# Four graph layers on one NeuronCore: the running count along an adjacency row as one scan of 1024 columns instead of two of 512

## Chip, cores and metric

The kernel runs on one core of a Trainium2 chip. The metric is the device time of one execution in microseconds, as the median of several runs. One further execution was recorded by the hardware profiler. Engines are named as the profile names them: PE is TensorE's matmul, PEld its weight load, DVE is VectorE, ACT is ScalarE, POOL is GpSimd, and SP is SyncE, which here only issues DMAs.

## What is computed

Sixteen graphs of 1024 nodes with 128 features pass through four layers, each followed by a residual sum and a layer norm: masked attention (layer 0), an edge convolution that takes a maximum over the neighbours (layer 1), a graph isomorphism layer (layer 2), and three SAGE convolutions on a "dilated" adjacency (layer 3). The change is in the dilation, which depends on the adjacency alone:

```python
def step(carry, n):                      # n = 0 .. 1023, one graph
    row = jnp.take(carry, n, axis=0)
    nbi = row.astype(jnp.int32)
    num = jnp.sum(nbi)
    sf = jnp.where(num > T_DIL, (num + K_DIL - 1) // K_DIL, 1)   # T_DIL 10, K_DIL 2
    rank = jnp.cumsum(nbi)
    rm = row & (rank % sf == 0)
    valid = (mask_b[n] != 0) & (num > 1)
    rm = jnp.where(valid, rm, False)
    keep = ~rm
    carry = carry.at[n].set(row & keep)
    carry = carry.at[:, n].set(carry[:, n] & keep)
    return (carry, None)
```

Rows are treated in order, and what a row removes is removed from the column too, so it affects the rows that follow. `rank` is the running count of neighbours along the row.

## The kernel before

**The main loop.** Layers 0 to 2 and the dilation run in one loop of 16 x 86 = 1376 slots of two half-slots each. Layer 1 sets its frame. The neighbours' maximum is computed over groups of six neighbours by tables of all subsets. In `slot`, each half-slot does the same: `look_up` (L779) multiplies a table by one-hot columns into the PSUM tile `pg`, which has two buffers; `count` (L748, L749) prepares the one-hot columns of two slots later on PE and ACT; every second slot `table` and `low_part` (L760 to L770) prepare tables; and DVE takes the running maximum, `nc.vector.tensor_max(own, own, pg)` (L831), which sets a buffer of `pg` free.

**The order.** The instructions of PE, ACT, DVE and POOL are put down in the order in which this Python loop emits them. The layers' other work is written as generators ("streams") that ask for an engine with an estimated cost; `advance` lets them emit when that engine's account has room. The account of DVE gains 1.1 a half-slot up to 2.2. A request that gives a PSUM bank back, or that is marked urgent (the subset tables, `tables_of`, L463 and L467), goes ahead whatever the account says. After the streams, in the same half-slot, the dilation is asked for its next step if it is due (L816 to L819); its cost is taken off DVE's account. The maximum of the half-slot comes last.

**The dilation** (L481 to L683) treats rows in 32 blocks of 32. Partition `g*32 + r` holds row `r` of the block in four graphs (`Q` = 4), so that a block is `E[128, 4, 1024]` in 8-bit integers. For each block:

- `rest` and `low_counts` (L601, L603) start a chain of 31 steps on GpSimd (L616 to L626) that decides row by row, for the 16 graphs, what the rows of the block remove among themselves. The chain yields 1.03 slots a step and hands out one item of other work for DVE with each: `yield 1.03, next(work, 0), False` (L627). When the items run out, the steps go on without any.
- The items are those of `behind`, which is `remove` of the block before, and then those of `prepare` for the next block. `prepare` (7 items) cuts squares out of the next rows, subtracts the columns that were removed before (`gone_T`) and counts.
- The chain's result goes through DRAM (`hit`, `hit_p`, L631 to L636). Some 8.8 slots after the last step, DVE transposes it (`hit_T`, L639), takes it out of `E`, and computes each row's count and three factors, `centre`, `scale` and `width` (L640 to L658). Then follow the columns that the next block needs at once (L660 to L678), and the next block's sums (L587 to L603).

`remove` (L549 to L576) does the removal along whole rows. For each of the four row groups `q` it makes the running count (`rank`) on DVE by two scans, the second starting at the last value of the first; ACT turns the count into |scale * rank + centre| in place (L564); DVE compares that with `width` and multiplies by the row (`gone`, L567); SP writes `gone` to DRAM (`removed`, L569); DVE transposes it in 32 x 32 blocks (`last_T`, L572), and SP writes that to DRAM too (`removed_T`, L574). `gone` of row group q-1 comes after the scans of row group q. Each scan, each `gone` and each transpose is an item of its own: 16 a block. `rank` and `gone` have two buffers each.

**After the loop** come the last items of `remove`, the end of layer 2 for the last graph, and layer 3, whose edges are read from `removed` (`load_edges`).

Of the kernel before, what the change touches and what calls it, by code (L numbers as in the profile page):

```python
# [35 lines left out]
ALU = mybir.AluOpType  # L36
# [35 lines left out]
def tile_graph_layers(ctx: ExitStack, tc, a, out):  # L72
    nc = tc.nc
    x, adj, adjT = a["x"], a["adj"], a["adjT"]
    halves = (slice(0, 512), slice(512, 1024))
# [91 lines left out]
    for b in range(B):  # L167
        q, g = divmod(b, G)
# [67 lines left out]
    def layers_012():  # L236
# [244 lines left out]
        def dilation():  # L481
# [67 lines left out]
            def remove(k, E, centre, scale, width):  # L549

                nonlocal last_T
                own = slice(k * R, (k + 1) * R)
                after = K - 2 - k
                if after > 0:
                    last_T = dil.tile([P, Q, after, R], BF, name="last_T")
                ranks = [None] * Q
                for q in range(Q + 1):
                    if q < Q:
                        rank = ranks[q] = dil.tile([P, N], F32, name="rank", bufs=2)
                        for h, s in enumerate(halves):  # L560
                            nc.vector.tensor_tensor_scan(rank[:, s], E[:, q, s], E[:, q, s],
                                                         rank[:, 511:512] if h else 0.0, op0=ALU.add, op1=ALU.max)
                            yield 1.3
                        nc.scalar.activation(rank, rank, AF.Abs, bias=centre[:, q:q + 1], scale=scale[:, q:q + 1])  # L564
                    if q:
                        gone = dil.tile([P, N], BF, name="gone", bufs=2)
                        nc.vector.scalar_tensor_tensor(gone, ranks[q - 1], width[:, q - 1:q], E[:, q - 1, :],  # L567
                                                       op0=ALU.is_equal, op1=ALU.mult)
                        nc.sync.dma_start(out=removed[k, :, q - 1, :], in_=gone)  # L569
                        yield 1.3  # L570
                        if after > 0:
                            nc.vector.transpose(last_T[:, q - 1].rearrange("p k r -> p (k r)"), gone[:, (k + 2) * R:])  # L572
                            if after > 1:
                                nc.sync.dma_start(out=removed_T[k + 3:, :, q - 1, own].rearrange("k p r -> p k r"),  # L574
                                                  in_=last_T[:, q - 1, 1:])
                            yield 0.8  # L576
# [5 lines left out]
            for k in range(K):  # L582
                E, V, _, counts = this
# [76 lines left out]
                if k + 1 < K:  # L660
# [18 lines left out]
                    yield 0.5, 2.6, False  # L679
                    this = following  # L680
                behind = remove(k, E, centre, scale, width)
            for cost in behind:
                yield 0.5, cost, False  # L683
# [486 lines left out]
```

## Time and profile before

| what | value |
|---|---|
| median of 3 runs | 6616.1 us (6615.68 to 6616.88) |
| profiled execution, its own time | 6613.2 us |
| span of its instructions | 6611.5 us |
| main loop, from the first running maximum to the end of the last | 137.3 to 5281.4 us |
| running maxima (L829 and L831) | 2752 |
| scans of 512 columns (L561) | 256 |

The profile's page gives for each engine its busy time, its share of the span and its number of instructions, and then the span in 40 slices with the busy share of each in tenths (9 is 90% or more); a slice here is 165 us. A group's row has the line, the engine, the operation, output and inputs, the shape and the count; then its busy time in us and the mean of one instruction in ns; then the engine's idle time before these instructions in us, and what ended it. In the source view of one line the durations are minimum, median and maximum in ns, followed by the first and last start in us. The waits view has who waited for whom, the total in us, how often, and the longest. The timeline has start and length in us; `x2` are two instructions in a row, merged; idle time before it stands in brackets. The stretches view has the busy time of each engine in given stretches of the span, and their sum and mean.

### The profile page before, as it was taken

The numbers are of one execution on the slowest core, as the hardware profiler recorded it, in microseconds if no ns is written. First come the engines' busy times: TensorE is split into PE (matmuls) and PEld (weight loads), VectorE is DVE, ScalarE is ACT, GpSimd is POOL, SyncE is SP. The second block draws the span as 40 slices with busy tenths as digits, with TensorE's granted clock in tenths as the row PEclk, the third lists the DMA queues.
The fourth block names the chain that finished last, engine by engine and source line by source line (L and its number), as shares of the span: only waits on it lengthen the run. The fifth ranks groups of instructions, "written<-read, shape, count | busy, mean of one in ns | idle before, by whom it ended". The sixth has DMA issues, their size and how long they took to land. (4 is left out here: it accounts for less than half of the span.)

```text
span 6611.5 us, 85916 instructions
## 1 busy us (share of the span) xinstructions
PE 5697.7 (86%) x27306; PEld 2883.8 (44%) x27306; DVE 5317.7 (80%) x8130; ACT 3733.9 (56%) x6537; POOL 3844.7 (58%) x11285
## 2 busy tenths in 40 slices
PE   6989898989898989899888898888888768787986
PEld 3434344444444444444444444444443345555643
DVE  3989899999999999999999999999998834444453
ACT  4656566666666666666666656666655523333841
POOL 2675767676767776766666676767676511110126
PEclk8989898989898989898989899999987779888997
DMA  5121212121212121212112212121110156563635
GB/s 37 14 27 22 30 24 36 20 27 26 28 28 27 27 27 26 28 26 31 28 29 30 27 26 27 26 27 28 25 25 9 32 93 120 105 124 102 230 128 166
DMA packets 478381, 317.02 MB, mean 48 GB/s; under 512 B 301162, under 2 KB 429668, under 8 KB 473828
## 3 DMA queue, kind: packets, MB, share of 16 engines
q0 software_dynamic: 105648, 84.20, 14.6%
q1 hardware_dynamic: 367600, 226.13, 11.7%
q8 instruction: 214, 3.51, 0.2%
q10 hardware_dynamic: 4676, 1.19, 0.1%
q14 instruction: 243, 1.99, 0.1%
HBM read 412.71 MB, written 117.18 MB: 80 GB/s over the span
## 5 line engine op out<-in xcount | busy, mean ns | idle before, releaser
L831 DVE TENSOR_TENSOR best<-best,pg 128x1024 f32<-128x1024 f32 x2720 | 3234.4, 1210 | 309.0 <-PE pg L779 300.5
L749 ACT ACTIVATE hot<-pm,one_less 128x512 fp32r<-128x512 f32 x2752 | 1882.3, 688 | 1115.1 <-PE pm L748 1102.9
L779 PE MATMUL pg<-hot,high 64*128 64x512 f32 x5504 | 1479.1, 534 | 453.6 <-DVE best L831 417.8
L779 PE MATMUL pg<-hot,low 64*128 64x512 f32 x5504 | 1173.3, 423 | 0.0
L748 PE MATMUL pm<-AT,lit 120*128 120x512 fp8e4 x2752 | 1143.8, 416 | 9.3 <-ACT hot L749 6.2
L779 PEld LDWEIGHTS pg<-hot,high 64*128 64x128 f32 x5504 | 547.9, 196 | 1265.1 <-DVE best L831 792.4
L616 POOL TENSOR_SCALAR sc<-low_counts,half_mask,rest 16x1 f32<-16x1 f32 x992 | 435.7, 439 | 399.6 <-DVE rest L603 305.8
L779 PEld LDWEIGHTS pg<-hot,low 64*128 64x128 f32 x5504 | 573.4, 205 | 0.0
L748 PEld LDWEIGHTS <-lit 120*128 120x128 fp8e4 x2752 | 274.5, 100 | 624.8 <-issue 560.8
L621 POOL TENSOR_SCALAR sc<-sc 16x1 f32<-16x1 f32 x992 | 430.1, 434 | 105.0
L770 ACT CAST low<-pt 128x256 fp32r<-128x256 f32 x688 | 255.6, 371 | 396.3 <-PE pt L768 392.1
L980 POOL TENSOR_TENSOR length<-length,mhalf 128x8 f32<-128x8 f32 x48 | 78.9, 1644 | 571.7 <-DVE length L979 571.7
L618 POOL TENSOR_SCALAR sc<-sc 16x1 f32<-16x1 f32 x992 | 341.8, 345 | 107.7
L624 POOL TENSOR_SCALAR last_rank<-V,sc 16x31 f32<-16x31 bf16 (+30 forms) x992 | 387.1, 390 | 0.0
L623 POOL TENSOR_SCALAR hit<-V,sc 16x31 bf16<-16x31 bf16 (+30 forms) x992 | 372.5, 376 | 0.0
L768 PE MATMUL pt<-high,less 128*128 128x256 f32 x688 | 303.2, 441 | 66.3 <-ACT high L763 58.9
L467 DVE TENSOR_TENSOR sub<-sub,q 128x24 f32<-128x24 f32 (+11 forms) x768 | 306.6, 400 | 24.6 <-ACT q L289 10.5
L619 POOL TENSOR_SCALAR sc<-sc 16x1 f32<-16x1 f32 x992 | 270.1, 272 | 83.3
L937 ACT CAST m<-near 128x1024 fp32r<-128x1024 fp8e4 x256 | 253.3, 1044 | 112.7 <-DVE near L906 59.8
L760 PE MATMUL pt<-ident,sub 128*128 128x128 f32 x1376 | 293.9, 298 | 24.7 <-ACT hot L749 22.0
L377 PE MATMUL pav<-v,eT 128*128 128x128 f32 x2048 | 307.6, 296 | 2.1 <-ACT eT L370 2.1
L617 POOL TENSOR_SCALAR sc<-sc 16x1 f32<-16x1 f32 x992 | 256.6, 259 | 86.6
(258 smaller groups left out, 9495.7 us busy)
## 6 DMA issues: line engine op xcount, KB each, us to landing
removed<-gone SPq DMA_DIRECT2D x128, 256.0 KB
An<-in_adj_dram POOLq DMA_DIRECT2D x16, 1024.0 KB, 15.1
E<-in_adj_dram POOLq DMA_DIRECT2D x128, 128.0 KB, 6.8
gone_all<-removed POOLq DMA_DIRECT2D x64, 256.0 KB, 12.1
near<-in_adjT_dram POOLq DMA_DIRECT2D x16, 1024.0 KB, 17.3
h<-x SPq DMA_DIRECT2D x32, 512.0 KB
kept<-near SPq DMA_DIRECT2D x16, 1024.0 KB
share<-share SPq DMA_DIRECT2D x32, 512.0 KB
```

What stands on the lines that cost most here:

```text
L377: nc.tensor.matmul(pav, eT[:, c, :], values[b][:, c, :], start=(c == 0), stop=(c == T - 1))
L467: nc.vector.tensor_max(sub[:, :n_g, n:2 * n], sub[:, :n_g, 0:n], qg[:, 2 * g0:2 * g0 + n_g, k:k + 1].to_broadcast([P, n_g, n]))
L616: gp.tensor_scalar(half, mine, half_mask[:, m], rest[:, n:n + 1], op0=ALU.mult, op1=ALU.add)
L618: gp.tensor_scalar(sf, half, 5.5, sf, op0=ALU.is_gt, op1=ALU.mult)
L621: gp.tensor_scalar(to, at, sf, none, op0=ALU.subtract, op1=ALU.subtract)
L623: gp.tensor_scalar(hit[:, n, n + 1:], V[:, n, n + 1:], at, None, op0=ALU.is_equal)
L624: gp.tensor_scalar(last[:, n + 1:], V[:, n, n + 1:], to, None, op0=ALU.is_le)
L748: nc.tensor.matmul(pm, lit[:, r, :], AT[b * (T + 1) + c][:, halves[h]], start=True, stop=True)
L749: nc.scalar.activation(hots[s][:, halves[h]], pm, AF.Relu, bias=one_less)
L768: nc.tensor.matmul(pt, less, high, start=False, stop=True, skip_group_check=True)
L779: nc.tensor.matmul(pg[:, a], part[rows, at * P:(at + 1) * P], hots[s][rows, halves[h]], start=(k == 0), stop=(k == 1))
L831: nc.vector.tensor_max(own, own, pg)
```

## The change

In `remove`, the two scans over 512 columns, each an item of its own with a cost of 1.3, become one scan over 1024 columns with a cost of 2.3. The scan of a row group starts at zero, and there is no second one that reads the first one's last value. Nothing else is changed.

```diff
                 for q in range(Q + 1):
                     if q < Q:
                         rank = ranks[q] = dil.tile([P, N], F32, name="rank", bufs=2)
-                        for h, s in enumerate(halves):
-                            nc.vector.tensor_tensor_scan(rank[:, s], E[:, q, s], E[:, q, s],
-                                                         rank[:, 511:512] if h else 0.0, op0=ALU.add, op1=ALU.max)
-                            yield 1.3
+                        nc.vector.tensor_tensor_scan(rank, E[:, q, :], E[:, q, :], 0.0, op0=ALU.add, op1=ALU.max)
+                        yield 2.3
                         nc.scalar.activation(rank, rank, AF.Abs, bias=centre[:, q:q + 1], scale=scale[:, q:q + 1])
```

## Prediction

> **What bounds the kernel now.** I read the page first, then the dilation's own line, then the timeline of the main loop, then stretches of it, then the waits. Durations are in us unless marked ns.
>
> ```profile
> PE 5697.7 (86%) x27306; PEld 2883.8 (44%) x27306; DVE 5317.7 (80%) x8130; ACT 3733.9 (56%) x6537; POOL 3844.7 (58%) x11285
> PE   6989898989898989899888898888888768787986
> DVE  3989899999999999999999999999998834444453
> L831 DVE TENSOR_TENSOR best<-best,pg 128x1024 f32<-128x1024 f32 x2720 | 3234.4, 1210 | 309.0 <-PE pg L779 300.5
> ```
>
> The DVE row holds 8 or 9 from the second slice to the 32nd: the main loop, 137 to 5281 us, with 2752 half-slots, each with one running maximum (L831). DVE and PE are both near full there, so which of them waits has to be read by stretch. The dilation works in 32 blocks of 85.4 half-slots. I cut 26 of them (blocks 4 to 29) at three marks of the timeline: from `rest` (L603) to the last handed-out step of `remove` and `prepare`; from there to `hit_T` (L639); from there to the next `rest`. The sums of the three answers of the stretches view:
>
> ```profile
> core 0: us, PE busy (x) PEld busy (x) DVE busy (x) ACT busy (x) POOL busy (x), PEclk, DMA share, GB/s
> ...
> sum 2302.40, PE 2059.16 PEld 992.65 DVE 2226.55 ACT 1431.48 POOL 1938.40; mean PE 79.20 PEld 38.18 DVE 85.64 ACT 55.06 POOL 74.55
> ...
> sum 1505.30, PE 1414.78 PEld 680.49 DVE 1275.71 ACT 1047.22 POOL 962.21; mean PE 54.41 PEld 26.17 DVE 49.07 ACT 40.28 POOL 37.01
> ...
> sum 350.90, PE 234.13 PEld 111.37 DVE 332.70 ACT 115.95 POOL 22.80; mean PE 9.00 PEld 4.28 DVE 12.80 ACT 4.46 POOL 0.88
> ```
>
> By the starts of the maxima these hold 1176, 911 and 133 half-slots. In the **item stretch** DVE is busy 97%: 1.958 us a half-slot, idle (2302.4 - 2226.6) / 1176 = 0.064. In the **free stretch**, where the dilation gives DVE nothing, PE is busy 94% and DVE 85%: 1.652 us a half-slot, idle (1505.3 - 1275.7) / 911 = 0.252. So DVE sets the pace while it has items, and TensorE when it has none. The waits of DVE in the main loop say the same, and name a third bound:
>
> ```profile
> DVE best L831 <- PE pg L779: 300.5, 571, 6.7
> DVE hit_T L639 <- DMA hit_p<-hit: 54.2, 9, 11.1
> ```
>
> Nine blocks end in a wait for `hit_p`, the result of GpSimd's chain of 31 steps (L616 to L626). The timeline shows one:
>
> ```profile
> 2641.97 18.79 DVE L831 TENSOR_TENSOR best<-best,pg 128x1024 f32<-128x1024 f32 x16 [0.47 <-PE pg L779]
> 2666.51 0.31 DVE L639 STREAM_TRANSPOSE hit_T<-hit_p 128x128 bf16<-128x128 bf16 x1 [5.75 <-DMA hit_p<-hit]
> ```
>
> DVE runs sixteen maxima and then stands 5.75 us. In those blocks neither DVE nor PE decides, but the chain (2524.9 to 2654.8 in this one, by GpSimd's timeline) and some 11 us of DMA behind it. The nine are odd blocks; the even ones have some 12 us to spare there.
>
> **What the Trainium skill says.** "DVE: opcode table, instruction layouts, handler registers and perf-mode slots", section "6. Datapath and trigger behaviour": the built-in scan runs at half throughput. The trace agrees: (1206 - 425) ns over 384 more elements (rows below) is 2.03 ns an element, twice the 1.04 of a 0.96 GHz clock ("VectorE: DVE Perf Modes", section "Specifications"). "Perfetto Trace Analysis", section "Optimizing Scalar/DVE Operations": an instruction on SBUF carries about 60 ns, larger operations help a saturated engine, and where DVE isn't saturated but makes bubbles elsewhere, breaking instructions up helps. Both halves of that bear here. "SBUF — State Buffer", section "Who interferes with whom": a DVE instruction with two SBUF inputs shuts out a GpSimd instruction that reads SBUF, for its whole length. The trace agrees: the chain's L617 has a median of 224 ns and a longest of 1365, and such long ones lie in scans.
>
> **The change, part by part.** The rows of the old scans, one of a short scan, and a piece of timeline:
>
> ```profile
> L561 DVE TENSOR_TENSOR_SCAN rank<-E x128: 1195/1206/1275, 292.6 to 5258.6; 128x512 f32<-128x512 uint8 x128
> L561 DVE TENSOR_TENSOR_SCAN rank<-E,rank x128: 1255/1275/1330, 295.8 to 5260.8; 128x512 f32<-128x512 uint8 x128
> L668 DVE TENSOR_TENSOR_SCAN at_columns<-running,near_columns x31: 423/425/426, 285.6 to 5099.4; 128x128 f32<-128x128 bf16 x31
> ```
>
> ```profile
> 2531.95 1.21 DVE L561 TENSOR_TENSOR_SCAN rank<-E 128x512 f32<-128x512 uint8 x1
> 2533.08 2.32 DVE L831 TENSOR_TENSOR best<-best,pg 128x1024 f32<-128x1024 f32 x2
> 2535.32 1.27 DVE L561 TENSOR_TENSOR_SCAN rank<-E,rank 128x512 f32<-128x512 uint8 x1
> 2536.52 2.32 DVE L831 TENSOR_TENSOR best<-best,pg 128x1024 f32<-128x1024 f32 x2
> ```
>
> (1) DVE time. The next instruction starts before a scan's recorded end: a first half occupies DVE for 2533.08 - 1.95 = 1.13, a second for 2536.52 - 5.32 = 1.20. No scan of 1024 is in the trace. I add 512 elements at 2.03 to 2.08 ns to the first half's 1.13: 2.17 to 2.20; I take 2.20. A pair then saves 1.13 + 1.20 - 2.20 = 0.13 (ends: 0.13 and, by recorded durations, 0.22). Four pairs a block: **-0.52**.
>
> (2) Four half-steps fewer. The chain hands out one item with each of its steps, 1.03 slots or 2.06 half-slots apart. `remove` has 16 items a block and will have 12; `prepare` keeps its 7. Block boundaries don't move, because the 31 steps and the waits after them are fixed in slots. So 4 x 2.06 = 8.24 half-slots a block pass from the item stretch (45.2 a block) to the free one (35.0). Work saved on DVE turns into time saved only where DVE decides, and these half-slots now go at TensorE's pace. At the idle rates above this adds 8.24 x (0.252 - 0.064) = +1.55. Against it, the shortened item stretch is denser (its mean item is larger), so its idle may fall: 37 half-slots x up to 0.02 = -0.74. Sum with (1): +0.29 to +1.03; I take **+0.75** a block that DVE and PE decide.
>
> (3) The long scan itself. Queued behind it on DVE is one maximum, and behind that PE's look-up two half-slots later, since `pg` has two buffers. PE fills both and stands a microsecond longer. That is free while DVE is the later of the two, as it is among items; the cover gone, each long scan costs up to its second half, 1.07.
>
> (4) GpSimd. By the timeline an operation of the chain caught in a scan loses on average 0.956 of the scan's 1.24, that is all but 0.285. Two halves cost 1.91, one scan of 2.26 would cost 1.975: +0.06, four times a block: **+0.25** where the chain decides.
>
> (5) At no cost: the Abs on ACT (1.23 us) gets its whole row at once, and `gone` still comes a slot (3.5 us) or more after it. The DMAs of `removed` and `removed_T` on SP come one step earlier per row group after the first; SP stood waiting for `gone` 2012.9 us in all, so nothing queues before them. If they piled up, only `gone`'s two buffers would feel it, 3 steps apart. The planner books 2.3 instead of 2.6 for DVE; its running-maximum and table streams don't look at that account. After the last block the rest of `remove` shrinks from 12 half-slots to 8: about +1, as PE decides the four freed.
>
> Sum: 31 blocks run `remove` inside them. 22 x 0.75 = 16.5; the nine that wait for `hit_p`: 9 x 0.25 = 2.3; the end 1. Together +20 on the profiled execution's 6613.2 (span 6611.5 and 1.7 around it): 6633. The median of the runs is 2.9 higher: **6636**.
>
> **Rivals.** (R1) Faster. If the freed half-slots have so little matmul work that PE passes them at DVE's pace, no idle is added, and (1) stands alone: 22 x 0.52 = 11, by durations 22 x 0.88 = 19; 6597 to 6605, say 6600. It decides below the idle x at which -0.52 + 8.24 (x - 0.064) = 0, x = 0.127, half of what the free stretch shows. The sixteen maxima above (1.17 apart) speak for it; but that is the end of an odd block, after PE's other work has run out, and the freed half-slots lie at the beginning of the stretch. The nine blocks bound by GpSimd give no gain. (R2) Both cancel: the denser item stretch returns all of the idle, 6618. (R3) Much slower: PE is busy 89% of the item stretch too; if PE loses 0.4 of the extra 1.07 in each of 124 long scans and doesn't recover it, +50: 6666. Against it: DVE's idle there is 0.064 a half-slot.
>
> **The numbers.** My forecast 0.55, with its own range of 6622 to 6658; R1 0.08; R2 0.25; R3 0.12. About 0.2% (13 us) is what a measurement can tell from no change. R2, and 0.05 of my forecast's lower edge, lie within it: same 0.30; slower 0.62; faster 0.08. The range of 8 in 10 takes R2, part of R1 and part of R3: 6606 to 6662.
>
> **What would show it.** Scans: x128, near 2.26 us, 2.20 to the next start. DVE busy less by 17 to 28 in all. In the same cut of stretches: some 37 half-slots of items and 43 free ones a block, free idle near 0.25, item idle 0.04 to 0.06, and DVE's wait for `pg` up from 300 by about 35. The longest of the chain's GpSimd operations about 2.3 us. I am wrong if the free idle falls below 0.13 (faster), if the item stretch's idle rises (R3), or if the scan's time isn't linear in its length.

## The result, and the profile after

The changed kernel takes 6673.9 us (median of 4 runs, 6668.4 to 6676.4) against 6616.5 for the kernel before on the same chip: a ratio of 1.0092, 95% interval 1.0078 to 1.0105. The forecast was 6636 with a range to 6662: the sign was right, and the loss is almost three times the one forecast. The profiled execution took 6676.4 us, with a span of 6674.7.

The page after (line numbers behind the scan are two lower than before):

```profile
PE 5719.4 (86%) x27306; PEld 2892.4 (43%) x27306; DVE 5319.2 (80%) x8002; ACT 3742.4 (56%) x6537; POOL 3873.8 (58%) x11285
...
L829 DVE TENSOR_TENSOR best<-best,pg 128x1024 f32<-128x1024 f32 x2720 | 3239.7, 1211 | 387.6 <-PE pg L777 375.2
```

DVE runs 128 instructions fewer and is no less busy (5317.7 before). Its idle time before the running maxima rose from 309.0 to 387.6, nearly all of it a wait for `pg`. The source view of the scan, and the sums of the same three cuts of blocks 4 to 29 (items, free, end of block):

```profile
L560 DVE TENSOR_TENSOR_SCAN rank<-E x128: 2262/2272/2361, 292.2 to 5321.1; 128x1024 f32<-128x1024 uint8 x128
```

```profile
sum 1912.50, PE 1674.49 PEld 787.00 DVE 1839.14 ACT 1143.09 POOL 1623.53; mean PE 64.40 PEld 30.27 DVE 70.74 ACT 43.97 POOL 62.44
...
sum 1910.20, PE 1770.16 PEld 865.93 DVE 1613.24 ACT 1301.49 POOL 1299.18; mean PE 68.08 PEld 33.31 DVE 62.05 ACT 50.06 POOL 49.97
...
sum 406.70, PE 290.88 PEld 140.52 DVE 383.88 ACT 157.74 POOL 22.78; mean PE 11.19 PEld 5.40 DVE 14.76 ACT 6.07 POOL 0.88
```

The scan is what was forecast, and so are the half-slots of the first two stretches, 35.4 and 43.5 a block by the starts of the maxima. But the idle of the item stretch rose from 0.064 to 0.080 a half-slot, and the third stretch, which the change wasn't thought to touch, grew from 350.9 to 406.7 us with the number of its half-slots, from 133 to 168. So I took the time of each block from the timeline, from one `spread` to the next:

| block | before | after | change |
|---|---|---|---|
| 3 | 167.1 | 157.6 | -9.5 |
| 5 | 153.4 | 176.2 | +22.8 |
| 7 | 154.2 | 171.2 | +17.0 |
| 9 | 155.9 | 175.7 | +19.8 |
| the 27 others of blocks 0 to 30 | | | +12.3 in all |

Three blocks (5, 7 and 9) carry +59.6 of the +62.4. Here is the beginning of block 5 in the timeline, before:

```profile
933.75 0.26 DVE L590 TENSOR_TENSOR spread<-counts,of_graph 128x96 f32<-128x96 f32 x1
933.92 2.35 DVE L831 TENSOR_TENSOR best<-best,pg 128x1024 f32<-128x1024 f32 x2
936.19 0.17 DVE L601 COPY low_counts<-pc 16x32 f32<-16x32 f32 x1
```

and after:

```profile
925.32 0.26 DVE L588 TENSOR_TENSOR spread<-counts,of_graph 128x96 f32<-128x96 f32 x1
...
950.43 0.18 DVE L599 COPY low_counts<-pc 16x32 f32<-16x32 f32 x1 [0.39 <-PE pc L595]
...
950.63 2.27 DVE L560 TENSOR_TENSOR_SCAN rank<-E 128x1024 f32<-128x1024 uint8 x1
```

From `spread` to `low_counts` it is 2.4 us before and 25.1 after, 15 half-slots instead of 2. No engine waits there for long: the bracket shows 0.39 us in which DVE stood idle for the matmul into `pc`. The wait lies in the order itself: between the two, the dilation asks for a bank of the shared PSUM pair (`pc`). The two banks are handed out in turn, and when the planner wrote the order down, the one whose turn it was had gone to a long sum for layer 2 (`pa`, L419). PE's timeline has the 24 matmuls of that sum ahead of those of `pc`, and in between short uses of the banks by streams that the planner asks before the dilation:

```profile
925.49 1.47 PE L419 MATMUL pa<-An,parts 128*128 128x512 fp8e4 x6
...
941.41 0.82 PE L419 MATMUL pa<-An,parts 128*128 128x512 fp8e4 x3
...
949.80 0.52 PE L595 MATMUL pc<-of_row,spread 128*16 128x32 f32 x12
```

In blocks 7 and 9 such a sum stands at the same place. The chain on GpSimd starts that much late. The planner's due times don't move with it, so that the next steps are emitted one a half-slot instead of one in two, until they have caught up. Sixty half-slots on, this is what it does to the engines. Pieces of the timelines of GpSimd, of ACT and of PE, and a line of the waits from 1030 to 1060 us:

```profile
1035.14 0.30 POOL L616 TENSOR_SCALAR sc<-sc 16x1 f32<-16x1 f32 x1
1037.70 0.20 POOL L220 TENSOR_TENSOR ln_mv<-ln_st 128x8 f32<-128x8 f32 x1
```

```profile
1041.30 1.65 ACT L270 ACTIVATE X<-y,ln_mv 128x128 f32<-128x128 f32 x4 [10.03 <-POOL ln_mv L228]
```

```profile
1043.58 0.69 PE L758 MATMUL pt<-ident,sub 128*128 128x128 f32 x2 [10.40 <-ACT hot L747]
```

```profile
DVE best L829 <- PE pg L777: 16.6, 7, 10.8
```

A layer norm (`ln_mv`, L220 to L228) stands on GpSimd behind steps of the chain that were emitted in a clump. ACT, in order, reaches the norm's result 10 us early and stands; the one-hot columns behind it on ACT are late; PE stands 10.4, DVE 10.8. In blocks 7 and 9 ACT stands 10.2 and 11.3 us for `ln_mv`, and in each of the three blocks a second time, for 2.6 to 3.3. This wait over the main loop, before and after:

```profile
ACT X L270 <- POOL ln_mv L228: 9.5, 3, 7.7
...
ACT X L270 <- POOL ln_mv L228: 48.5, 7, 11.3
```

The six waits of blocks 5, 7 and 9 make up some 41 us; what else the three blocks lose wasn't followed to single waits. They have 88.7 us of DVE idle between them, against 32.0 before; in the whole main loop it rose by 66.5.

### The profile page after: what moved, and what is told of

Same layout as the page of the kernel before. It is cut to its first block, busy times and chain, and to the rows that moved or that the text cites. A ratio compares the mean times of both kernels' runs of the same rounds, so it can differ in the third digit from the quotient of the medians.

```text
span 6674.7 us, 85818 instructions
## 1 busy us (share of the span) xinstructions
PE 5719.4 (86%) x27306; PEld 2892.4 (43%) x27306; DVE 5319.2 (80%) x8002; ACT 3742.4 (56%) x6537; POOL 3873.8 (58%) x11285
## 5 line engine op out<-in xcount | busy, mean ns | idle before, releaser
L829 DVE TENSOR_TENSOR best<-best,pg 128x1024 f32<-128x1024 f32 x2720 | 3239.7, 1211 | 387.6 <-PE pg L777 375.2
L614 POOL TENSOR_SCALAR sc<-low_counts,half_mask,rest 16x1 f32<-16x1 f32 x992 | 460.8, 465 | 445.0 <-DVE rest L601 350.9
L619 POOL TENSOR_SCALAR sc<-sc 16x1 f32<-16x1 f32 x992 | 429.4, 433 | 105.0
L616 POOL TENSOR_SCALAR sc<-sc 16x1 f32<-16x1 f32 x992 | 345.0, 348 | 107.7
L622 POOL TENSOR_SCALAR last_rank<-V,sc 16x31 f32<-16x31 bf16 (+30 forms) x992 | 365.6, 369 | 0.0
L617 POOL TENSOR_SCALAR sc<-sc 16x1 f32<-16x1 f32 x992 | 299.0, 301 | 83.3
L467 DVE TENSOR_TENSOR sub<-sub,q 128x24 f32<-128x24 f32 (+11 forms) x768 | 310.1, 405 | 24.4 <-ACT q L289 10.5
L615 POOL TENSOR_SCALAR sc<-sc 16x1 f32<-16x1 f32 x992 | 257.3, 259 | 86.5
## 6 DMA issues: line engine op xcount, KB each, us to landing
gone_all<-removed POOLq DMA_DIRECT2D x64, 256.0 KB, 12.3
```

Of the source, the lines that this page charges most:

```text
L467: nc.vector.tensor_max(sub[:, :n_g, n:2 * n], sub[:, :n_g, 0:n], qg[:, 2 * g0:2 * g0 + n_g, k:k + 1].to_broadcast([P, n_g, n]))
L614: gp.tensor_scalar(half, mine, half_mask[:, m], rest[:, n:n + 1], op0=ALU.mult, op1=ALU.add)
L616: gp.tensor_scalar(sf, half, 5.5, sf, op0=ALU.is_gt, op1=ALU.mult)
L619: gp.tensor_scalar(to, at, sf, none, op0=ALU.subtract, op1=ALU.subtract)
L622: gp.tensor_scalar(last[:, n + 1:], V[:, n, n + 1:], to, None, op0=ALU.is_le)
```

## Experiments

Theory **L** (late blocks): three blocks start their chain late because of the order that the planner wrote. Theory **S**: the prediction's R3, the long scan starves TensorE. Ratios are to the kernel before on the same chip, with their 95% interval. "Late" gives the half-slots by which `pc` is delayed beyond the usual one. Block times are of the profiled executions. (Some of the expectations count one half-slot more.)

| kernel | late (block: half-slots) | ratio |
|---|---|---|
| before | 3: 8, 9: 1, 11: 2 | 1 |
| after | 5: 13, 7: 12, 9: 13 | 1.0092 (1.0078 to 1.0105) |
| e1_booked_28 | none | 1.0040 (1.0026 to 1.0054) |
| e2_halves_one_step | as after | 1.0109 (1.0095 to 1.0123) |
| e3_long_two_steps | as before | 1.0033 (1.0020 to 1.0046) |
| e4_booked_13 | as before | 1.0034 (1.0021 to 1.0046) |
| e5_before_booked_17 | 5: 10, 7: 12, 9: 12 | 1.0031 (1.0019 to 1.0042) |
| e6_before_booked_20 | none | 1.0027 (1.0016 to 1.0038) |
| e7_late_odd | 13, 15, 17: 13 each | 1.0127 (1.0112 to 1.0143) |
| e8_late_even | 14: 13, 16: 14, 18: 15 | 1.0140 (1.0126 to 1.0154) |
| e9_gone_transpose_one | as before | 1.0041 (1.0029 to 1.0054) |
| e10_bank_kept | none | 1.0011 (1.0004 to 1.0017) |
| e11_before_booked_16 | 9: 1, 11: 2 | 0.9980 (0.9973 to 0.9987) |
| e12_long_second_step | as before | 1.0026 (1.0017 to 1.0035) |

**e1_booked_28**, one number in the changed kernel:

```diff
-                        yield 2.3
+                        yield 2.8
```

> The changed kernel with one number different: the scan of 1024 is booked at 2.8 instead of 2.3 on the planner's account of DVE. Same instructions, other order; the dilation's request for a PSUM bank (pc, L595) is then met at once in every block, where in the changed kernel blocks 5, 7 and 9 wait 13 to 14 half-slots for it. Theory L (late blocks): those three blocks take 176.2, 171.2 and 175.7 us against 153.4, 154.2 and 155.9 before, together +59.6, so this kernel should give nearly all of that back: 6612 to 6622. Theory S (the long scan starves TensorE, rival R3 of the prediction): the 124 long scans are all there, so 6665 to 6680.

1.0040, 6643 us on this chip. More than half of the loss is gone with all long scans in place, which S can't explain; but some 0.3% more is left than L had expected. Blocks 5, 7 and 9 are within 3 us of before; the even blocks hold +21.6.

**e2_halves_one_step**, the changed kernel with its scan undone and its order kept:

```diff
-                        nc.vector.tensor_tensor_scan(rank, E[:, q, :], E[:, q, :], 0.0, op0=ALU.add, op1=ALU.max)
+                        for h, s in enumerate(halves):
+                            nc.vector.tensor_tensor_scan(rank[:, s], E[:, q, s], E[:, q, s],
+                                                         rank[:, 511:512] if h else 0.0, op0=ALU.add, op1=ALU.max)
                         yield 2.3
```

> Two scans of 512 as in the kernel before, but both in one item booked at 2.3: the order of everything else is that of the changed kernel, with the three late blocks, and only the long scan is undone. Theory L: no better than the changed kernel, 6670 to 6690 (0.13 us more DVE time a pair, at most 17 in all). Theory S as the single long instruction: back to 6620 to 6635. (S as any 2.3 us of DVE work in one half-slot can't be told from L here; e1 and e3 do that.)

1.0109: no better than the changed kernel; the two intervals overlap. Short scans don't help where the order stays. Blocks 5, 7 and 9 are late by the same half-slots and cost +60.3.

**e3_long_two_steps**, the long scan with the order of before:

```diff
-                        yield 2.3
+                        yield 1.3
+                        yield 1.3
```

> One scan of 1024 booked at 1.3, followed by an empty item booked at 1.3: 16 items a block as before, so the order of all other instructions is that of the kernel before. Only the long scan is left of the change. Theory L: the 0.13 us a pair is saved in the blocks that DVE decides, -8 to -17: 6600 to 6609. Theory S: slower than before by most of the 57 us, 6650 to 6675.

1.0033, a miss of both theories. Block 1 alone is +15.6. The timeline of SP's queue there:

```profile
421.68 0.38 SPq L573 DMA_DIRECT2D removed_T<-last_T  x1
422.10 19.13 SPq L634 DMA_DIRECT2D hit_p<-hit  x1
```

The last of four `hit_p` DMAs is issued behind `removed_T`, whose 128 x 29 pieces have 64 bytes each, and its issue takes 19.13 us; DVE waits 22 us for `hit_p`. (Its place in the order doesn't explain the length: the other issues right behind a `removed_T` in this run took 3.3 us at most.) The order on SP isn't among those written down by hand, and it came out differently here. Without block 1, +12 is left.

**e4_booked_13**, the changed kernel with the banks late where they were before:

```diff
-                        yield 2.3
+                        yield 1.3
```

> The changed kernel with its scan booked at 1.3: one item a row group, but the bank is late in the same three blocks as in the kernel before (3, 9 and 11, by 9, 2 and 3 half-slots) and not in 5, 7 and 9. This is the change with its order's accident taken away, and tests the prediction's own sum: +20, 6636 (6625 to 6645). Theory S: 6665 to 6680.

1.0034: +22 us, inside what the prediction's sum had given. With the accident of its order taken away, the change costs about what was forecast, most of it in the even blocks (+23.2 of +28.5).

**e5_before_booked_17**, the kernel before with another number and no other instruction:

```diff
-                            yield 1.3
+                            yield 1.7
```

> The kernel before, with each of its two scans of 512 booked at 1.7 instead of 1.3 on the planner's account: no instruction is changed, only the order. By this booking the bank for pc comes late in blocks 5, 7 and 9 (11, 13 and 13 half-slots), and no longer in block 3. Theory L (late blocks cost some 20 us each where the chain on GpSimd decides): three times 17 to 20, less 9 in block 3: +42 to +51 on the kernel before, a ratio of 1.0063 to 1.0078. Theory S (the long scan): no change, within 0.2%.

1.0031, half of what was expected. The part that was to be tested came: blocks 5, 7 and 9 are +14.7, +18.0 and +16.9, together +49.6, with ACT's wait among its lines again:

```profile
ACT X L270 <- POOL ln_mv L228: 32.9, 7, 8.0
```

(9.5 before.) Block 3 gave back 12.0, as expected, but the others gave back 16 more, which wasn't.

**e6_before_booked_20**, the same with 2.0.

> The kernel before with each scan of 512 booked at 2.0: no bank comes late in any block. Theory L: block 3 alone gives back its 9 us and blocks 9 and 11 one or two each: -8 to -13, a ratio of 0.998 to 0.9988, unless the streams' later DVE work costs it elsewhere. Theory S: no change.

1.0027, wrong in sign. No bank is late, block 3 gives back 7.8, and the even blocks lose 26.4 (10 and 12 some 8 each). A higher booking moves the streams' DVE work too; that this is the price, of the same size as in e1, isn't shown.

**e7_late_odd** and **e8_late_even** hold the dilation of e6 back by 7 slots in three blocks:

```diff
+                hold_to = now + 7.0 if k in (13, 15, 17) else 0.0
                 yield 0, 0.9, True
...
-                if s >= 0 and due <= now and not (wants_bank and taken >= 2 and given.get(taken - 2, 1e9) > now):
+                if s >= 0 and max(due, hold_to) <= now and not (wants_bank and taken >= 2 and given.get(taken - 2, 1e9) > now):
```

and (14, 16, 18) in the other.

> The kernel of the run booked at 2.0, in which the dilation is held back after spread by 7 slots in blocks 13, 15 and 17, so that their chain on GpSimd starts 13 half-slots late; what follows catches up one item a half-slot. Nothing else is moved by the planner's banks. In odd blocks the chain decides the end (hit_T came 11 to 14 us after the chain's end before). Theory L with the chain as the bound: 13 half-slots of 1.6 us, some 20 us a block: +55 to +65 on that run. If late blocks cost only through DVE and TensorE (13 half-slots moved from the idle-free stretch to one with idle 0.25): 3 a block, +10.

> The same hold of 7 slots in blocks 14, 16 and 18 (late by 13, 14 and 15 half-slots). In even blocks hit_T came 20 to 25 us after the chain's end, of which the DMAs need 11, so some 12 us are to spare. With the chain as the bound: 22 to 24 us late less 12, some 10 to 12 a block: +30 to +36 on the run booked at 2.0, about half of the odd blocks' cost. Without the chain as the bound: the same as in the odd blocks.

Against e6, blocks 13, 15 and 17 of e7 are +23.8, +23.3 and +23.5, and the others are -5.8 in all: a late block costs its lateness. ACT's waits for `ln_mv` are 13.5 to 17.4 us of it in each of the three. But blocks 14, 16 and 18 of e8 are +18.2, +21.8 and +29.0. That the chain's end sets the time, with 12 us to spare in even blocks, falls. Waits of e8 from 2440 to 2482 us:

```profile
DVE best L833 <- PE pg L781: 23.2, 2, 22.4
ACT parts L408 <- POOL left L411: 22.8, 1, 22.8
PE pm L750 <- ACT hot L751: 21.9, 1, 21.9
```

In the even blocks it isn't the layer norm that stands behind the clump on GpSimd but layer 2's subtraction (`left`, L411), and the same three engines stand 22 us for it. In blocks 16 and 18 ACT's wait is 25.8 and 30.1 us, so that this one wait is at least as long as what the block loses. In the even blocks wholly, and in the odd ones for the larger part, GpSimd's queue decides: whoever needs a small result of it waits until the clumped steps are through.

**e9_gone_transpose_one**, the freed half-slots alone, in the kernel before:

```diff
-                        yield 1.3
+                        if after < 1:
+                            yield 1.3
                         if after > 0:
...
-                            yield 0.8
+                            yield 1.3
```

> The kernel before with its two scans of 512, but each comparison (gone) and its transpose as one item booked at 1.3: 12 items a block, as in the changed kernel, with no long scan. Banks come late where they do in the kernel before (blocks 3, 9 and 11). This is the prediction's step (2), freed half-slots, alone. If freed half-slots cost what the run booked at 1.3 has over the run with an empty item (about 16 us without the latter's 15.6 us in block 1): +16 to +25, a ratio of 1.0024 to 1.0038. If they are free: at most 1.001.

1.0041, just above what was expected. Twelve items instead of sixteen cost 0.7 us a block (+21.6 in 31 blocks of the profiled execution), with short scans; it is the even blocks that lose (+24.3), while the odd ones are at -2.7. Its first two stretches have 957 and 1130 half-slots (1176 and 911 before):

```profile
sum 1971.20, PE 1735.45 PEld 822.61 DVE 1916.69 ACT 1189.85 POOL 1669.53; mean PE 66.75 PEld 31.64 DVE 73.72 ACT 45.76 POOL 64.21
...
sum 1858.00, PE 1753.44 PEld 857.87 DVE 1599.26 ACT 1291.87 POOL 1237.22; mean PE 67.44 PEld 32.99 DVE 61.51 ACT 49.69 POOL 47.59
```

The free idle is (1858.0 - 1599.3) / 1130 = 0.229 a half-slot, the item idle 0.057.

**e10_bank_kept**, the changed kernel with the cause taken away:

```diff
-                            or take and taken >= 2 and given.get(taken - 2, 1e9) > now
+                            or take and (wants_bank or taken >= 2 and given.get(taken - 2, 1e9) > now)
```

> The changed kernel, scan of 1024 booked at 2.3, with one more condition in the planner: no stream takes a PSUM bank of the shared pair while the dilation's request for one stands. pc then comes at once in all blocks. Theory L: the 59.6 us of blocks 5, 7 and 9 go, all the rest of the changed kernel stays (its other blocks were +3.1 in sum): 6617 to 6635, a ratio of 1.0002 to 1.003. Theory S, or another cause: still near 1.009.

1.0011: as L had it. All long scans are there, all half-slots are freed, and 0.8% of the 0.92% is gone. Blocks 5, 7 and 9 are +3.6 together. The granted clock of TensorE isn't what did it: its mean over these runs is 0.903, and 0.906 over those of the kernel before on this chip. The waits for `pg`:

```profile
DVE best L829 <- PE pg L777: 322.7, 613, 10.4
```

(375.2 in the changed kernel, 300.5 before.)

**e11_before_booked_16**: the kernel before with 1.6 for 1.3.

> The kernel before with each scan of 512 booked at 1.6: block 3 is no longer late, the small delays of blocks 9 and 11 stay. Theory L: -8 to -14 on the kernel before, a ratio of 0.9979 to 0.9988, if the rest of the order does not lose it again, as it did in the run booked at 2.0.

0.9980: 6599 us beside 6612 on this chip, faster than both kernels. Block 3 gives -12.1 of the -16.6 in the profiled execution.

**e12_long_second_step**: as e3, with the empty item ahead of the scan.

```diff
+                        yield 1.3
                         nc.vector.tensor_tensor_scan(rank, E[:, q, :], E[:, q, :], 0.0, op0=ALU.add, op1=ALU.max)
-                        yield 1.3
                         yield 1.3
```

> The long scan alone, as in the run with the empty item, but with the empty item first and the scan second. In that run the last of the four hit_p DMAs of block 1 stood 19 us behind a removed_T DMA on SP's queue (block 1 was +15.6); in this one that DMA comes after hit_p, as in the kernel before. If that was it: 15 us less than that run, +0 to +12 on the kernel before, a ratio of 1.000 to 1.0018. If the long scan itself costs: as that run, 1.0033.

1.0026. Block 1 is at -0.6, so the DMA on SP was its cause in e3; but the scan alone still costs 0.26%, above the range. Its item stretch, with 1175 half-slots:

```profile
sum 2322.80, PE 2056.77 PEld 993.28 DVE 2218.67 ACT 1431.56 POOL 1958.47; mean PE 79.11 PEld 38.20 DVE 85.33 ACT 55.06 POOL 75.33
```

DVE is busy 7.9 us less than before and idle 104.1 instead of 75.8: 0.089 a half-slot for 0.064, a quarter of a microsecond for each long scan.

## Why the prediction was wrong

The step that failed is in (2): "Block boundaries don't move, because the 31 steps and the waits after them are fixed in slots", with its companion in (5), that the planner's booking costs nothing because two kinds of stream "don't look at that account". The steps are fixed, but the chain's start isn't: it waits, at the time of planning, for a PSUM bank. The new booking, 2.3 once for 1.3 twice, moved other streams' requests by some half-slots, and in blocks 5, 7 and 9 a long sum of layer 2 then had the bank whose turn it was. That is 59.6 of the 62.4 us in blocks 0 to 30. It is shown from three sides: gone with the bank kept (e10), there without any long scan (e2) and without any change of instructions (e5, +49.6 in the three blocks), and made at will in other blocks (e7, e8).

(1) The scan: right. 2272 ns, and 2201 to the next start, where 2.20 had been taken; in DVE's timeline the scans' share fell by 17.4 us. Yet DVE's busy time didn't fall "by 17 to 28": the maxima's share rose by 10.3 and the tables' (L467) by 4.2. A part of that is how busy time is counted. A maximum's last 0.08 us (1216 ns with idle behind it, 1132 to the next start without) lie under the next instruction, and count where DVE then stands idle; 683 maxima have idle behind them instead of 612, which is 6 us.

(2) The freed half-slots: right in mechanism and roughly in size. The gross cost was put at 1.55 less up to 0.74 of idle a block; e9 gives 0.70 by itself.

(3) The long scan was put at nothing while DVE is the later of the two. It costs: 0.26% in e12, even after its saving. The idle that was to fall in the denser item stretch rises, from 0.064 to 0.080 a half-slot in the changed kernel and to 0.082 in e10. That was a sign named for being wrong. e9, with short scans, is at 0.057.

(4) GpSimd: operations caught in a scan lost some 236 us in all before and 253 after, by what each took beyond the median of its line and shape. That is 0.14 a pair instead of 0.06: a long scan costs 2.04 and not 1.975. The sign named for it, a longest operation of about 2.3, could tell nothing: L616 reached 2288 ns before the change already (2581 after). The whole chain, without the first and last block, takes 128.7 before and 129.6 in e12, four times the 0.25 that was forecast.

(5) ACT now waits 43.0 us for the scan instead of 5.0; in e10 that wait is 33.9 us at a ratio of 1.0011, so it isn't the loss.

R3 had forecast 6666 and so came near in number, but by luck and not by its mechanism: e10 has every long scan and loses 0.11%. It holds in small, as (3).

What stays open: the parts don't add up. e9 and e12 cost 0.41% and 0.26% by themselves, both together in e4 0.34% and in e10 0.11%. e10 has +16.3 us in its even blocks too, but gets 9.3 back in block 3, whose bank was late before. e1 and e6, without a late block, lose 0.3 to 0.4%, most of it in their even blocks. Each of them has an order of its own, and what in it costs this wasn't looked into.

A rival for this rest is the clock that TensorE was granted. Its mean in the profiled execution is 0.904 before, 0.897 in the changed kernel, 0.899 in e1 and 0.897 in e6, against 0.905 in e12 and 0.908 in e10; PE is busy 5718.5 us in e1 for the matmuls that took 5697.7 before. Whether a lower clock made these kernels slower, or their order lowered the clock, isn't shown. For the late blocks it can be a part at most: from 1040 to 1060 us, around the end of ACT's wait in block 5, the clock is at 0.50, but e5 has its +49.6 in the same three blocks at a mean of 0.903.

## What to carry to other kernels

Where a program writes out the order of its engines by a plan with booked costs, an edit has two effects: what it does on the chip, and what it does to the plan. Print the plan of both versions, here the half-slot in which each block gets its bank, ahead of pricing instructions; an experiment that alters a booking alone, or keeps the order while it alters the instruction, separates the two. And look at what stands behind a burst on an in-order queue: a small operation on an engine that is busy 58% of the time stopped ACT, PE and DVE for ten to thirty microseconds.

## What the runs showed of the hardware

A scan of 1024 takes 2272 ns, 1066 more than the first of 512: 2.08 ns an element. Behind a DMA of 64-byte pieces (`removed_T`, 128 x 29 of them), the issue of the next on the same queue once took 19.13 us, where the median of that DMA is 0.43; with the order turned round in e12, block 1 lost nothing. Why it was so long stays open. And a late start of 13 to 15 half-slots cost 18 to 29 us, whether or not the late chain itself had time to spare.
